# An FFN with per-batch mixing: two loads on another queue, one application moved into the next step, the last product regrouped by PSUM bank

## The chip, the core and the metric

The kernel runs on one core of a Trainium2 chip. A core has five engines that run their own instruction streams: TensorE (PE in the profile; its weight loads are PEld), VectorE (DVE), ScalarE (ACT), GpSimd (POOL) and SyncE (SP). SP only issues transfers here; ACT and POOL can issue them too. The metric is device time in microseconds of one launch. Before the change the median of three runs is 420.22 us (418.6 to 420.79).

## The reference

For every one of 64 batches a 64x64 matrix is picked by an index and applied across the channels; the result goes through a dense 1024x1024 layer and through a low-rank branch of the expert that a gate chooses for each token; the input is added at the end.

```python
W = weights[condition]                       # 64 of 16 matrices, each 64 x 64
h = einsum('bct,bcd->bdt', x, W)             # x: 64 x 64 x 1024
h = h.reshape(-1, 1024)                      # 4096 tokens
logits = h @ gate_w.T + expert_bias          # 4 experts
one_hot = onehot(argmax(logits))
base = h @ W_up.T
z = einsum('nh,erh->ner', h, lora_A)         # rank 8
delta = einsum('ner,ehr,ne->nh', z, lora_B, one_hot)
out = x + base + delta
```

All inputs and outputs are float32.

## The kernel before

The 4096 tokens are 32 pieces of 128 rows (two batches each). The picked matrices mix rows, and the dense weights mix columns, so the kernel does the weights first: u = x W for the joined weights W of 1024 x 1060 columns (4 gate columns, 32 of the experts' A, 1024 of W_up; `NW`, `G` = 36 is the first 36), and then, in PSUM tiles called `o`, the block-diagonal matrix `bd` of the two batches times u. This second product is the "application" (`apply`, `cond_u`). It is done in column pieces (`COLS`: 354, 354, 352); the first piece holds the gate columns, from which `gate` works out the chosen expert's 32 numbers `z` on DVE in six small instructions. `turn` transposes `z` on PE and splits it into `zt`, `delta` adds the low-rank part to an application's piece by one more matmul, and `evict` takes the piece out of PSUM. `finish(i, j)` is `apply`, `delta` and `evict` of piece j of token piece i.

Full float32 accuracy is made from reduced-precision operands: every operand is split into a high part (a copy on ACT: `ah`, `hB`, `hT`, `uh`) and a low part (a subtraction on DVE: `al`, `lB`, `lT`, `ul`), and each product is three matmuls: high x high, high x low, low x high.

Two token pieces a = 2g and b = 2g+1 are one group. W is cut into a 2 x 2 grid of blocks B11 to B22 (512 rows by 530 columns, `NB`), x of a group into A11, A12 (piece a) and A21, A22 (piece b). Groups 0 and 1 do the 8 block products as they are (`eight`); groups 2 to 15 do 7 products with sums of blocks (`seven`: S1 to S4 of A, T1 to T4 of B). A block product is four chunks k = 0 to 3 (`KH`) of six matmuls: three for columns 0 to 263 (`CUT`) and three for columns 264 to 529, in the two banks of a PSUM tile `c` (three tiles, `chain`). Two one-bank tiles `o` are left for applications and transposes (`place`).

The order of work on PE, DVE, ACT and POOL is the order in which the program is written (`InOrder`, line 41; nearly every instruction has that line). It is written as a list of block products per group, and hooks `at(s, k, fn, ...)`: after chunk k of product s (k = -1: ahead of it) fn's instructions are put in. Transfers that SP issues are ordered by the framework's scheduler.

Three places matter here.

- The start (lines 348 to 397). Group 0's A11 and A21 are loaded together, in two transfers of `load_halves` into a tile `xx`: chunk 0 (`ONE`, 128 KB) on ACT's queue, chunks 1 to 3 (`REST`, 384 KB) on SP's, which comes behind the two halves of chunk 0 of B11 (line 387) and ahead of the chunks 1 to 3 of B11 (`load_b`, line 139). Short dummy matmuls (`keep_warm`) stand ahead of chunk 0 and between chunks 0 and 1 and 1 and 2.
- The seam between group 1 and group 2. `apply(a, 0)` and `gate(a)` of group 1's piece a stand after the last chunk of the last product of group 1 (lines 551, 552); `u_of(pb, 0, ...)`, the split of piece b's u, ahead of group 2's first product (line 593), `turn` after its chunk 2, and `delta` and `evict` after chunk 0 of the second product.
- The end, group 15 (lines 659 to 707). Its order of products is such that only S4 x B22 is left for the columns 530 to 1059 of piece a. This product writes one two-bank tile `c["5"]`. In its hooks stand `turn(b)` and the pieces 0 and 1 of piece b; behind it come the sums for piece a's second half in two pieces (178 and 352 columns), and `finish(b, 2)`, `finish(a, 1)`, `finish(a, 2)`. For the last two token pieces (a = 30, b = 31) x is loaded ahead into the tile `y` (`load_y`), `evict` adds to it on DVE, and each of the six column pieces is stored by its own transfer on SP. For all other pieces `evict` copies on ACT, POOL issues a transfer that adds x into `y`, and SP stores the whole piece of 512 KB.

Of the kernel before, what the change touches and what calls it, by code (L numbers as in the profile page):

```python
# [17 lines left out]
KH = KC // 2  # L18
# [7 lines left out]
LEFT = 512 - CUT  # L26
COLS = ((0, 354), (354, 354), (708, 352))
WARM = 27
GATE = (("lg", E), ("mx", 1), ("sc", E), ("m2", 1), ("zm", ER))
# [15 lines left out]
def kernel(  # L45
# [140 lines left out]
    def chain():  # L186
        return psum.tile([P, 1024], F32, name="c", tag="c", bufs=3)

    def product(g, which, hooks):

        for k in range(KH):
            for c, a, b, first in which:
                h, lo = As[g, a]
                for o, n in (
                    (c[:, LEFT:512], slice(0, CUT)),
                    (c[:, 512 : LEFT + NB], slice(CUT, NB)),
                ):
                    for m, (l, r) in enumerate(((h, wh[b]), (h, wl[b]), (lo, wh[b]))):
                        tensor.matmul(
                            o,  # L200
                            l[:, k],
                            r[:, k, n],
                            start=first and k == 0 and m == 0,
                            stop=k == KH - 1 and m == 2,
                            skip_group_check=True,
                        )
            for kk, fn, *args in hooks:
                if kk == k:
                    fn(*args)

    def body(c):
# [19 lines left out]
    def u_of(i, hf, c):  # L231
        u_split(i, half(hf), body(c))

    def u_add(i, c, t):
        s = ts["u", i] = temp("usum")
        vector.tensor_add(s, body(c), t)
# [13 lines left out]

    def load_y(i):
        ys[i] = yp.tile([P, H], F32, name="y", tag="y")
        nc.sync.dma_start(ys[i], x[i])

# [15 lines left out]

    wide = []

    def place():
        if wide and wide.pop(0):
            return chain()[:, :512]
        return psum.tile([P, 512], F32, name="o", tag="o", bufs=2)
# [6 lines left out]

    def apply(i, j):
        c0, n = COLS[j]
        o = os_[i, j] = place()
        cond_u(o[:, :n], i, slice(c0, c0 + n))

    def ycols(j):
        c0, n = COLS[j]  # L290
        s = G if j == 0 else 0
        return slice(s, n), slice(c0 + s - G, c0 + n - G)
# [19 lines left out]

    def turn(i):
        zp = place()
        tensor.transpose(zp[: 3 * ER, :P], zs[i].rearrange("p a b -> p (a b)"), ident)
        zt = zs[i] = sp.tile([3 * ER, P], F32R, name="zt")
        scalar.copy(zt, zp[: 3 * ER, :P])
        p = slice(2 * ER, 3 * ER)
        vector.tensor_sub(zt[p], zp[p, :P], zt[p].bitcast(F32))

    def delta(i, j):
        s, d = ycols(j)
        tensor.matmul(
            os_[i, j][:, s], zs[i], b3[:, d], start=False, stop=True, skip_group_check=True
        )

    def evict(i, j):

        s, d = ycols(j)
        o = os_.pop((i, j))[:, s]  # L330
        if i >= NP - 2:
            vector.tensor_add(ys[i][:, d], o, ys[i][:, d])
            nc.sync.dma_start(out[i, :, d], ys[i][:, d])
            return
        if j == 0:
            ys[i] = yp.tile([P, H], F32, name="y", tag="y")
        scalar.copy(ys[i][:, d], o)
        if j == 2:
            pool.dma_start(ys[i], x[i], accum_op=ALU.add)
            nc.sync.dma_start(out[i], ys.pop(i))  # L340

    def finish(i, j):
        apply(i, j)
        delta(i, j)
        evict(i, j)
# [23 lines left out]
    ONE, REST = slice(0, 1), slice(1, KH)  # L369
    load_halves(scalar, 0, ONE)  # L370

    one = cpool.tile([P, 1], F32, name="one")
# [13 lines left out]
    for n in pieces:  # L386
        nc.sync.dma_start(t[:, n], part("B11", 0)[:, n])  # L387
    load_halves(nc.sync, 0, REST)
    for k in range(1, KH):
# [61 lines left out]
    def eight(g):  # L451
# [3 lines left out]
        def at(s, k, fn, *args):  # L455
            h[s].append((k, fn, *args))
# [6 lines left out]
        if g == 0:  # L463
            each(0, -1, load_b, "B12", range(KH))
            at(0, 0, keep_warm, 8)
            at(0, 0, split_a, g, "A11", REST)
# [58 lines left out]
        else:  # L525
# [24 lines left out]
            at(7, 0, sums, g + 1, "S4")  # L550
            at(7, 3, apply, a, 0)
            at(7, 3, gate, a)
            order = (
# [13 lines left out]
    def seven(g):  # L567
# [6 lines left out]
        def at(s, k, fn, *args):  # L574
            h[s].append((k, fn, *args))
# [9 lines left out]
        def gate_of_b():  # L585
            wide.append(True)
            o = place()
            cond_u(o[:, :G], b, slice(0, G))
            gate(b, o)
            u_split(b, slice(G, NB), ts["last"][:, G:])  # L590

        if g == 2:
            at(0, -1, lambda: u_of(pb, 0, cp["1"]))
            at(0, 2, turn, pa)
            at(1, 0, delta, pa, 0)
            at(1, 0, evict, pa, 0)
            at(1, 1, finish, pa, 1)
            at(1, 2, finish, pa, 2)
            for k in range(KH):
                at(1 + k, 3, split_b, "T4", k)  # L600
            at(1, 3, apply, pb, 0)
            at(1, 3, gate, pb)
            at(2, 3, turn, pb)
        else:
            at(0, -1, lambda: u_sum(pb, 0, cp["2"], ts["t1"]))
            at(0, 1, finish, pa, 1)
            at(0, 3, finish, pa, 2)
            at(1, 2, apply, pb, 0)
            at(1, 2, gate, pb)
            at(2, 2, turn, pb)  # L610
# [48 lines left out]
        else:  # L659
# [7 lines left out]
                ("3", "S1", "T1", True),  # L667
                ("5", "S4", "B22", True),
            )
# [12 lines left out]
            at(5, -1, first_of_b)  # L682
            at(5, 0, turn, a)
            at(5, 1, gate_of_b)
            at(5, 2, delta, a, 0)
            at(5, 2, evict, a, 0)
            at(6, -1, lambda: u_add(b, c["3"], ts["t7"]))
            at(6, -1, lambda: scalar.copy(us[b][0][:, half(1)], ts["u", b]))
            at(6, -1, lambda: keep_sum("t8", c["3"], "t6"))
            at(6, 0, turn, b)  # L690
            at(6, 0, lambda: u_low(b, half(1), ts["u", b]))
            for j in (0, 1):
                at(6, 2, finish, b, j)
        run(g, order, h, c)
        cs[g] = dict(c)
        if last:
            wide.extend((True, True, False))
            s = temp("usum")
            pieces = [slice(NB, 708), slice(708, NW)]
            for n in pieces:  # L700
                d = slice(n.start - NB, n.stop - NB)
                vector.tensor_add(s[:, d], body(c["5"])[:, d], ts["t8"][:, d])
                scalar.copy(us[a][0][:, n], s[:, d])
            for n in pieces:
                u_low(a, n, s[:, n.start - NB : n.stop - NB])
            for i, j in ((b, 2), (a, 1), (a, 2)):
                finish(i, j)

# [49 lines left out]
```

## Time and profile before

| | |
|---|---|
| median of three runs | 420.22 us |
| the profiled execution: its own time | 419.19 us |
| its span in the profile | 417.4 us |
| PE busy | 409.3 us (98%) |
| PEld busy | 406.6 us (97%) |
| DVE busy | 286.4 us (69%) |
| ACT busy | 186.4 us (45%) |
| POOL busy | 74.2 us (18%) |
| granted TensorE clock | 1.00 |
| read and written in HBM | 43.68 MB, 16.78 MB |

The span runs from the first to the last instruction that the profiler recorded; 1.8 us of the execution's time lie around it. All times of day below are microseconds from the span's start. In a row of the timeline the first number is the start, the second the duration (of the whole run of instructions if there are several, shown as x and a count), then the engine, the source line, the operation and its tiles (written <- read); in square brackets stands how long the engine sat idle before it and what ended that. A matmul's duration is from its issue until its result has drained; the next matmul is issued earlier (264 columns: 0.123 us later), so starts, not durations, are to be summed on PE.

### The profile page before, as it was taken

To read this page: it belongs to the slowest core of one execution; us is meant where nothing else is said; L and a number is where in the kernel's file an instruction comes from. 1 tells how busy PE (TensorE), PEld (TensorE's weight loads), DVE (VectorE), ACT (ScalarE), POOL (GpSimd) and SP (SyncE) were. 2 spreads that over 40 slices of the span, in tenths; PEclk is the share of its full clock that TensorE was granted. 3 is DMA by queue.
4 is the path that set the end of the run, shared out by engine and by line. 5 is a ranking of instruction groups with operands and counts; after the bars stand their busy time and mean duration, and the time that the engine had idled before them with its cause. 6 is when DMAs were issued, how large, how long until landed. Compare 5 with 4: busy or idle time off the path is not lost.

```text
span 417.4 us, 8151 instructions
## 1 busy us (share of the span) xinstructions
PE 409.3 (98%) x3195; PEld 406.6 (97%) x3195; DVE 286.4 (69%) x644; ACT 186.4 (45%) x418; POOL 74.2 (18%) x91
## 2 busy tenths in 40 slices
PE   6999999999999999999999999999999999999995
PEld 5999999999999999999999999999999999999994
DVE  4887685876757667676676767666676776767765
ACT  5747555453434445233453534335343444524521
POOL 5303512021020201102020020201102020020000
PEclk9999999999999999999999999999999999999999
DMA  7988983443655534564443555534365553474434
GB/s 247 321 281 208 236 204 74 113 142 118 177 132 133 122 80 155 133 176 121 103 123 102 172 133 153 124 82 145 116 178 133 128 121 83 157 197 113 91 63 151
DMA packets 25270, 60.99 MB, mean 146 GB/s; under 512 B 3248, under 2 KB 4784, under 8 KB 25232
## 3 DMA queue, kind: packets, MB, share of 16 engines
q1 hardware_dynamic: 18400, 41.39, 27.8%
q0 software_dynamic: 6560, 18.96, 26.7%
q8 instruction: 25, 0.41, 0.4%
q14 instruction: 13, 0.11, 0.1%
q10 hardware_dynamic: 272, 0.13, 0.1%
HBM read 43.68 MB, written 16.78 MB: 145 GB/s over the span
## 4 chain that ended last, share of the span: by engine, by line
PE 89%; DMA 3%; DVE 3%; issue 2%; ACT 1%; POOL 0%; SPq 0%; DVEq 0%; POOLq 0%; ACTq 0%
PE c L41 74%; PE o L41 15%; DMA wraw<-in_w_dram 3%; DVE lT L41 1%; POOL wraw L41 0%; ACT hT L41 0%; DVE S L41 0%; DVE al L41 0%; DVE ul L41 0%; ACT uh L41 0%; DVE usum L41 0%; DVE y L41 0%; SPq L387 0%; DVE lB L41 0%; DVE bd L41 0%
## 5 line engine op out<-in xcount | busy, mean ns | idle before, releaser
L41 PE MATMUL c<-hT,ah 128*128 128x264 f32 x480 | 139.8, 291 | 0.0
L41 PE MATMUL c<-hT,al 128*128 128x264 f32 x480 | 137.0, 286 | 0.0
L41 PE MATMUL c<-lT,ah 128*128 128x264 f32 x480 | 137.0, 285 | 0.0
L41 PE MATMUL c<-hB,ah 128*128 128x264 f32 (+1 forms) x432 | 124.3, 288 | 1.9 <-ACT hB L41 1.9
L41 PE MATMUL c<-lB,ah 128*128 128x264 f32 (+1 forms) x432 | 123.1, 285 | 0.4 <-DVE lB L41 0.4
L41 PE MATMUL c<-hB,al 128*128 128x264 f32 (+1 forms) x432 | 123.2, 285 | 0.0
L41 PEld LDWEIGHTS c<-lT,ah 128*128 128x128 f32 x480 | 90.9, 189 | 0.0
L41 PEld LDWEIGHTS c<-hT,ah 128*128 128x128 f32 x480 | 90.8, 189 | 0.0
L41 PEld LDWEIGHTS c<-hT,al 128*128 128x128 f32 x480 | 90.7, 189 | 0.0
L41 PEld LDWEIGHTS c<-hB,ah 128*128 128x128 f32 x432 | 81.6, 189 | 2.3 <-ACT hB L41 2.3
L41 PEld LDWEIGHTS c<-lB,ah 128*128 128x128 f32 x432 | 81.9, 189 | 0.8 <-DVE lB L41 0.8
L41 PEld LDWEIGHTS c<-hB,al 128*128 128x128 f32 x432 | 81.5, 189 | 0.0
L41 POOL DMA_DIRECT2D y<-in_x_dram x30 | 28.8, 959 | 283.9 <-ACT y L41 283.9
L41 ACT COPY y<-o 128x354 f32<-128x354 f32 (+2 forms) x90 | 39.7, 442 | 57.2 <-PE o L41 54.8
L41 ACT CAST uh<-usum 128x530 fp32r<-128x530 f32 (+4 forms) x44 | 27.1, 616 | 72.4 <-DVE usum L41 72.3
L41 DVE TENSOR_TENSOR al<-S,ah 128x512 fp32r<-128x512 f32 x56 | 38.5, 688 | 24.4 <-ACT ah L41 24.4
L41 DVE TENSOR_TENSOR al<-xh,ah 128x512 fp32r<-128x512 f32 x46 | 31.7, 689 | 29.9 <-ACT ah L41 29.9
L41 PE MATMUL o<-uh,bd 128*128 128x354 f32 (+1 forms) x188 | 45.7, 324 | 0.0
L41 DVE TENSOR_TENSOR ul<-usum,uh 128x530 fp32r<-128x530 f32 (+4 forms) x44 | 30.0, 683 | 18.8 <-ACT uh L41 18.8
L41 ACT CAST zt<-o 96x128 fp32r<-96x128 f32 x32 | 8.4, 261 | 75.4 <-PE o L41 75.2
L41 POOL DMA_INDIRECT wsel<-in_cw_dram,idx x32 | 34.6, 1081 | 11.6 <-issue 5.2
L41 ACT CAST ah<-S 128x512 fp32r<-128x512 f32 x56 | 34.9, 623 | 1.8 <-DVE S L41 1.4
(74 smaller groups left out, 461.0 us busy)
## 6 DMA issues: line engine op xcount, KB each, us to landing
xh<-in_xt_dram SPq DMA_DIRECT2D x60, 256.0 KB, 5.1
y<-in_x_dram POOLq DMA_DIRECT2D x30, 512.0 KB, 5.6
out_dram<-y SPq DMA_DIRECT2D x30, 512.0 KB, 2.9
wraw<-in_w_dram SPq DMA_DIRECT2D x23, 265.0 KB, 6.4
wraw<-in_w_dram POOLq DMA_DIRECT2D x8, 265.0 KB, 6.8
y<-in_x_dram SPq DMA_DIRECT2D x2, 512.0 KB, 4.5
xx<-in_xt_dram SPq DMA_DIRECT2D x1, 512.0 KB, 7.2
wsel<-in_cw_dram,idx POOLq DMA_INDIRECT x32, 5.0
```

Of the source, the lines that this page charges most:

```text
L41: return lambda *a, **k: self.tc.keep_in_program_order(fn(*a, **k))
```

## The change

- The start: `REST` of A11 and A21 goes on ACT's queue, right behind `ONE`. SP's queue then has chunks 1 to 3 of B11 right behind chunk 0. The eight dummy matmuls between chunks 0 and 1 become six.
- The seam: `apply(pa, 0)` and `gate(pa)` move behind chunk 0 of group 2's first product, `u_of(pb, 0)` with them (its place in the order of ACT and DVE stays), and `turn(pa)` from behind chunk 2 to behind chunk 3. On DVE the low part of `zt` now comes behind `al` of S1.
- The end: the last product is taken bank by bank: twelve matmuls of 264 columns into one `o` tile, then twelve of 266 into the other. Piece a is applied in four pieces (`LAST`: 354, 176, 264, 266 columns). Its first two are copied by ACT, POOL adds x to these 494 columns (`FIRST`) by a transfer, and SP stores them in one transfer, which stands ahead of the other five stores in SP's order. `turn(a)` goes from behind chunk 0 to behind chunk 1 of S1 x T1; `turn(b)` and the pieces of b use halves of the two-bank tiles.

```diff
+LAST = ((0, 354), (354, NB - 354), (NB, CUT), (NB + CUT, NB - CUT))
...
+    def product_by_bank(g, places, a, b, hooks):
+
+        for m, (o, n) in enumerate(zip(places, BANKS)):
+            for k in range(KH):
+                part_of_product(g, a, b, True, k, o[:, : n.stop - n.start], n)
+                for kk, fn, *args in hooks:
+                    if kk == KH * m + k:
+                        fn(*args)
...
     def load_y(i):
+
         ys[i] = yp.tile([P, H], F32, name="y", tag="y")
-        nc.sync.dma_start(ys[i], x[i])
+        d = slice(FIRST if i == NP - 2 else 0, H)
+        nc.sync.dma_start(ys[i][:, d], x[i][:, d])
...
-        if i >= NP - 2:
+        if i == NP - 1 or d.start >= FIRST and i == NP - 2:
             vector.tensor_add(ys[i][:, d], o, ys[i][:, d])
             nc.sync.dma_start(out[i, :, d], ys[i][:, d])
             return
-        if j == 0:
+        if i < NP - 2 and j == 0:
             ys[i] = yp.tile([P, H], F32, name="y", tag="y")
         scalar.copy(ys[i][:, d], o)
-        if j == 2:
+        if i == NP - 2 and j == 1:
+            n = slice(0, FIRST)
+            pool.dma_start(ys[i][:, n], x[i][:, n], accum_op=ALU.add)
+        elif j == 2:
...
     load_halves(scalar, 0, ONE)
+    load_halves(scalar, 0, REST)
...
-    load_halves(nc.sync, 0, REST)
...
-            at(0, 0, keep_warm, 8)
+            at(0, 0, keep_warm, 6)
...
-            at(7, 3, apply, a, 0)
-            at(7, 3, gate, a)
...
-            at(0, -1, lambda: u_of(pb, 0, cp["1"]))
-            at(0, 2, turn, pa)
+            at(0, 0, apply, pa, 0)
+            at(0, 0, gate, pa)
+            at(0, 0, lambda: u_of(pb, 0, cp["1"]))
+            at(0, 3, turn, pa)
...
-                ("5", "S4", "B22", True),
...
-            at(5, 0, turn, a)
+            at(5, 1, turn, a)
             at(5, 1, gate_of_b)
             at(5, 2, delta, a, 0)
             at(5, 2, evict, a, 0)
-            at(6, -1, lambda: u_add(b, c["3"], ts["t7"]))
-            at(6, -1, lambda: scalar.copy(us[b][0][:, half(1)], ts["u", b]))
-            at(6, -1, lambda: keep_sum("t8", c["3"], "t6"))
-            at(6, 0, turn, b)
-            at(6, 0, lambda: u_low(b, half(1), ts["u", b]))
-            for j in (0, 1):
-                at(6, 2, finish, b, j)
+            at(5, 3, lambda: finish(a, 1, ts["w"][:, 512:]))
...
+            z = chain()
+            turn(b, z[:, :512])
+            u_add(b, c["3"], ts["t7"])
+            scalar.copy(us[b][0][:, half(1)], ts["u", b])
+            keep_sum("t8", c["3"], "t6")
+            u_low(b, half(1), ts["u", b])
             s = temp("usum")
...
+            places = place(), place()
...
+            product_by_bank(
+                g,
+                places,
+                "S4",
+                "B22",
+                [
+                    (3, lambda: finish(b, 0, z[:, 512:])),
+                    (3, u_bank, 0),
+                    (5, lambda: finish(b, 1, chain()[:, :512])),
+                    (5, u_bank_low, 0),
+                ],
+            )
+            nc.sync.dma_start(out[a, :, :FIRST], ys[a][:, :FIRST])
+            u_bank(1)
+            finish(b, 2, chain()[:, :512])
+            u_bank_low(1)
+            finish(a, 2)
+            finish(a, 3)
```

`u_bank(m)` adds bank m to the kept sum `t8` on DVE and copies the high part on ACT; `u_bank_low(m)` makes the low part on DVE.

## The prediction

> **What bounds the kernel now.** I read the page's busy shares first, then the chain that ended last, PE's waits, and then the timeline around each wait.
>
> ```profile
> span 417.4 us, 8151 instructions
> PE 409.3 (98%) x3195; PEld 406.6 (97%) x3195; DVE 286.4 (69%) x644; ACT 186.4 (45%) x418; POOL 74.2 (18%) x91
> ...
> PE 89%; DMA 3%; DVE 3%; issue 2%; ACT 1%; POOL 0%; SPq 0%; DVEq 0%; POOLq 0%; ACTq 0%
> ```
>
> PE works nearly all the time at granted clock 1.00, and the change takes no real matmul away. So it can win only where PE stands still, and after PE's last matmul. PE's own waits, all of them:
>
> ```profile
> PE c L41 <- ACT hB L41: 1.9, 2, 1.6
> PE o L41 <- DVE one L41: 1.0, 1, 1.0
> PE o L41 <- DVE ul L41: 0.4, 1, 0.4
> PE c L41 <- DVE lB L41: 0.4, 1, 0.4
> PE c L41 <- ACT uh L41: 0.2, 1, 0.2
> ```
>
> The second is the launch. The first and fourth are the start, the third is the seam of groups 1 and 2 (at 60 us), the last the end. Each is touched by one part of the change. Everything from 61 to 400 us runs without a wait of PE.
>
> **Part 1, the start.** PE has done chunk 0 at 6.2 us and begins chunk 1 at 8.61, when ACT has made `hB`:
>
> ```profile
> 7.26 0.51 ACT L41 CAST ah<-xx 128x384 fp32r<-128x384 f32 x1 [2.48 <-DMA xx<-in_xt_dram]
> 7.93 0.63 ACT L41 CAST hB<-wraw 128x530 fp32r<-128x530 f32 x1 [0.16 <-DMA wraw<-in_w_dram]
> ```
>
> `REST` (issued at 1.65) lands at 7.25, chunk 1 of B11 (issued at 2.12) at 7.91. Both lie on SP's queue, and the stretches show the transfer engines far from full while they wait:
>
> ```profile
> 3.00:3.50 0.50, 0.50 (x7) 0.50 (x6) 0.00 (x0) 0.00 (x0) 0.50 (x3) 1.00 0.71 240
> 3.50:4.00 0.50, 0.50 (x6) 0.28 (x3) 0.01 (x1) 0.34 (x2) 0.50 (x3) 1.00 0.56 110
> 4.00:4.50 0.50, 0.23 (x2) 0.18 (x1) 0.48 (x2) 0.50 (x3) 0.50 (x6) 1.00 0.83 127
> 4.50:5.00 0.50, 0.42 (x2) 0.22 (x3) 0.50 (x3) 0.28 (x2) 0.30 (x1) 1.00 0.62 117
> 5.00:5.50 0.50, 0.50 (x5) 0.50 (x5) 0.28 (x2) 0.00 (x0) 0.00 (x0) 1.00 1.01 277
> ```
>
> (The last two columns are the engines' share and GB/s.) From 3.5 to 5.0 us they move 110 to 127 GB/s; from 6.5 on, 376 to 387. ACT's queue is empty in that time. Moved to it, `REST` is issued at 1.20 (behind `ONE`, 0.74 + 0.46) and chunk 1 at 1.65.
>
> Lower end of the gain: only the issue moves, 0.43 to 0.47 us, the duration of `REST`'s issue on SP. Upper end: two streams fill the gap. Chunk 0, `ONE`, `REST` and chunk 1 are 265 + 128 + 384 + 265 = 1042 KB; summed over the stretches they are through at about 6.45 us, 672 KB of them after 3.25; at 370 GB/s these take 1.8 us, to 5.1: 1.35 us earlier. Below zero: ACT takes `REST` ahead of `hB`, and if the four loads share the engines so that `REST` lands like the 512 KB load of the same tile (7.2 us after issue, 8.4), `hB` starts at 8.93 instead of 7.93: 1.0 us lost. I take 1.2: three loads are issued by then and the engines are half idle, so of all rows these point at the one queue itself, and the upper end is nearer. The second issue on ACT delays its table load (1.22 to 2.50) by 0.46, to 2.96; its first copy of data is at 3.66, so that costs nothing. The two dummy matmuls cost 0.11 us only if chunk 1 is ready before 6.9. Behind chunk 1 the nearest need is `lB` of B21's chunk 0 (done 12.9, used at 14.0), whose loads ride the same stream and come earlier with it.
>
> The Trainium skill ("DMA: Bandwidth & Descriptors", section "Issuing engines are not separate DMA queues") says that issuing on several engines saves only the sequencer's issue time, as all transfers run on the same 16 engines. By that rule this part is worth 0.45, and the sum at the end is 1.45 instead of 2.2.
>
> **Part 2, the seam.**
>
> ```profile
> 59.70 0.48 PE L41 MATMUL o<-uh,bd 128*128 128x354 f32 x2
> 60.56 0.43 PE L41 MATMUL o<-ul,bd 128*128 128x354 f32 x1 [0.38 <-DVE ul L41]
> 60.83 0.29 PE L41 MATMUL c<-hB,ah 128*128 128x264 f32 x1
> ```
>
> The application takes 59.70 to 60.83 = 1.13 us of PE, where one without a wait takes 0.49 (385.02 to 385.51). Behind chunk 0 (6 x 0.123 = 0.735) its `ul` matmul is due at 59.70 + 0.735 + 0.325 = 60.76; `ul` is there at 60.51. So 0.64 us go. Two things come back. `turn` now ends product 0 (63.13) and `delta` follows 0.85 later (0.115 for the transpose, 0.735 for a chunk); from transpose to `zt` took 0.90 (63.05 to 63.95) with DVE free, and now `al` of S1 is ahead of it until 63.7: about 0.1 of wait. Then `evict` copies that `o` tile later than PE wants it for `finish(pa, 1)`: ACT has the copy of `t` first (c's last result drains at 64.1, so it runs 64.17 to 64.77), the eviction ends at about 65.1, PE is due at 64.95: 0.2. Net 0.35; ends 0.64 (neither wait shows) and 0.1 (both double). The gate comes 0.1 later and its first user, `turn`, waits at 63.13 for a `z` done at 62.5: nothing.
>
> **Part 3, the end.** PE's last matmul is issued at 412.99, DVE's last `y` is
>
> ```profile
> 413.45 0.51 DVE L41 TENSOR_TENSOR y<-o,y 128x352 f32<-128x352 f32 x1
> ```
>
> and SP's last store is issued at 414.0. I follow the new order with before's durations, without the gains upstream. `turn(a)` waited for `z` at 403.14 (idle from 402.9); behind chunk 1 it does not: 0.25 won on PE. Product 5 ends at 405.70, `finish(a, 1)` at 406.12 (4 matmuls of 176 columns at some 0.1), where z of b is ready too (its gate, on DVE, is 0.07 later than before). Bank 0 is done at 407.72, `finish(b, 0)` 408.36, half of bank 1 409.10, `finish(b, 1)` 409.75, bank 1 410.49, `finish(b, 2)` 411.14. From here DVE sets the pace: low part of `zt` 406.9, the two sums of 530 (0.61 apart) from 407.2, `ul` 408.6, `y` 409.2, bank 0's sum 409.6, `y` 410.1, `ul` 410.55, bank 1's sum 410.9, `y` 411.5, `ul` 411.9 to 412.3, `y` 412.3, and the last `y` after the last `delta` at 412.8 to 413.2. That is 0.75 us before 413.96. The tail of stores is denser (five transfers within 2.3 us, 1.05 MB in all), which takes perhaps 0.1 back: 0.65 net. Ends: 0.85, and zero if the hand-offs of DVE, ACT and PE each cost a little more.
>
> The new store of 494 columns stands first in SP's order and waits for POOL's transfer; all five others queue behind it. ACT's second copy is done at 406.65, and POOL issues 0.3 later, at 406.95. The nearest row is the last such transfer of before:
>
> ```profile
> y<-in_x_dram POOLq DMA_DIRECT2D x1, 512.0 KB, 5.4
> ```
>
> It was issued at 401.14, and its data flowed from 403.4 to 406.1. With half the bytes: 2.2 to the first byte, 1.35 of data, 0.4 = 4.0 us, so 410.95. Six issues 0.37 apart put the last at 412.8 at the earliest, and its data are ready at 413.2: no cost. This cover ends when the transfer takes over 4.4 us. At 5.4 the last store is issued at 414.2, and the part wins nothing. The skill's same page (section "Anatomy of one DMA") gives 2.0 us plus the bytes at 436 GB/s for such a transfer, an estimate of 2.6 us here; for 512 KB it would give 3.2 where this trace shows 5.4, so the trace's row is used.
>
> **The sum.** 1.2 + 0.35 + 0.65 = 2.2 us. The profiled execution (419.19, 1.8 of it around the span) would take 417.0; it lies 1.0 below the median of the runs, and from that median, 420.22, I get 418.0.
>
> **The rivals.**
>
> 1. The second queue saves the issue time only. For it: `ONE`, on ACT's queue from 0.74 on, needed 2.9 us for 128 KB although little else was moving. Against: the half-empty engines. 0.45 + 0.35 + 0.65 = 1.45: 418.8.
> 2. `REST` suffers from sharing and lands at 8.4. For: it is the first that ACT needs, and chunks 1 to 3 now run beside it, not behind it. -1.0 + 0.35 + 0.65 = 0: 420.2.
> 3. The start's gain is lost at the seam. The chain that ended last runs through a POOL transfer of 8.1 us (41.79 to 49.91) and a DVE that is busy without a break from 55.8 to the `ul` at 60.51. If these do not come earlier with PE, all gain up to there is capped at 60.83 + 0.735 - 60.72 = 0.84, less 0.3: 0.55 + 0.65 = 1.2: 419.0. Against: POOL's issue at 41.2 follows ACT's work on PE's results, and the transfer engines were half idle at 28 to 32 us, so nothing older holds them.
> 4. The other side: POOL's addition lands late, and five stores stand behind it. In the crowded window from 30 to 62 us the same kind of transfer took
>
> ```profile
> y<-in_x_dram POOLq DMA_DIRECT2D x2, 512.0 KB, 9.7
> ```
>
> At 9.7 it lands at 416.65 and the last store is issued at 418.5 instead of 414.0: 4.5 - 1.2 - 0.35 = 2.95 slower, 423.2. From 5.2 us on the end loses; from 8.9 us on the whole is slower by over 0.5%. Against: at the end only stores run.
>
> **How the numbers follow.** 0.5% of the time is 2.1 us, about what a measurement of this kernel can tell from no change. Chances: forecast 0.53 (its own range 1.7 to 2.9 us, of which 0.07 lies within 0.5%), rival 1 0.18, rival 2 0.08, rival 3 0.06, rival 4 or something of its size 0.15. Faster by over 0.5%: 0.53 - 0.07 = 0.46. Within: 0.07 + 0.18 + 0.08 + 0.06 = 0.39. Slower: 0.15. The range goes from all upper ends (1.35 + 0.64 + 0.85 = 2.85, and 0.4 for the spread of the runs: 417.0) to rival 2 with 0.4 of spread (420.6); rival 4 is left out.
>
> **What would show it.** Part 1: `hB` of chunk 1 starts at about 6.7 instead of 7.93, and the stretches from 3.5 to 5.0 move over 250 GB/s. At about 7.5 it is rival 1, above 7.93 rival 2. Part 2: the wait on `ul` is gone, small ones on `zt` and on the `y` copy appear at 64 to 65 us (less the start's gain). Part 3: from the last product's first matmul to SP's last issue; SP's wait for POOL's transfer ends before DVE's second `y`. I am wrong if the start's gain does not reach 61 us, if POOL's last transfer takes over 4.4 us, or if PE shows a wait between 61 and 400 us.

## The result, and the profile after

| | before | after |
|---|---|---|
| median | 419.61 us (14 runs, 417.82 to 421.24) | 419.78 us (14 runs, 418.53 to 421.83) |
| ratio after / before | | 1.0009, 95% interval 0.9987 to 1.0031 |
| the profiled execution: its time, its span | 419.19, 417.4 us | 419.16, 417.4 us |

The change makes no difference that can be measured. The interval goes from 0.5 us faster to 1.3 us slower: the time lies inside the predicted range, and the gain of 2.2 us that was forecast is not there. The first lines of the page after, with the shares of the chain that ended last:

```profile
span 417.4 us, 8160 instructions
PE 409.8 (98%) x3197; PEld 407.1 (98%) x3197; DVE 285.6 (68%) x643; ACT 186.9 (45%) x420; POOL 75.5 (18%) x92
...
PE 90%; DMA 3%; DVE 2%; issue 2%; ACT 1%; POOL 0%; SPq 0%; POOLq 0%; DVEq 0%; ACTq 0%
```

and PE's waits (engine, tile and releaser: us in total, times, longest):

```profile
PE o L42 <- DVE one L42: 1.0, 1, 1.0
PE c L42 <- ACT hB L42: 0.8, 2, 0.4
PE c L42 <- DVE lB L42: 0.4, 1, 0.4
PE o L42 <- DVE ul L42: 0.3, 1, 0.3
```

The wait for `hB` went from 1.9 to 0.8, as part 1 meant. The wait for `ul`, which part 2 was to remove, is still there. (This list counts a wait from the modelled end of the matmul before; below, PE's waits are what lies between two starts beyond the usual distance.) To see where the 1.1 us of the start went, PE's timeline is cut at three matmuls that are the same in every version: number 100 and number 500 (counted from 0, without the dummies; about 20 and 71 us) and number 3080 (about 401 us, in the last group). From 500 to 3080 every execution but that of one variant takes 330.12 to 330.19 us, so all that differs is in three columns:

| | start: up to matmul 100 | seam: 100 to 500 | end: from 3080 to 0.05 us ahead of the span's end | span |
|---|---|---|---|---|
| before | 20.33 | 51.46 | 15.44 | 417.4 |
| after | 19.31 | 51.87 | 15.99 | 417.4 |
| difference | -1.02 | +0.41 | +0.55 | 0 |

**Start.** The stretches after (the last two columns are the transfer engines' share and GB/s) and ACT's timeline:

```profile
3.50:4.00 0.50, 0.50 (x6) 0.29 (x3) 0.00 (x0) 0.32 (x2) 0.50 (x3) 1.00 1.07 393
4.00:4.50 0.50, 0.19 (x2) 0.15 (x1) 0.47 (x2) 0.38 (x2) 0.50 (x6) 1.00 1.03 368
4.50:5.00 0.50, 0.42 (x2) 0.22 (x3) 0.40 (x2) 0.50 (x2) 0.30 (x1) 1.00 1.08 367
```

```profile
5.76 0.51 ACT L42 CAST ah<-xx 128x384 fp32r<-128x384 f32 x1 [0.73 <-DMA xx<-in_xt_dram]
6.91 0.63 ACT L42 CAST hB<-wraw 128x530 fp32r<-128x530 f32 x1 [0.64 <-DMA wraw<-in_w_dram]
```

The half-empty stretches are full, the split of `REST` starts 1.5 us earlier (5.76 for 7.26) and that of chunk 1 1.0 earlier (6.91 for 7.93).

**Seam.** PE's timeline at the application of group 1's piece a:

```profile
59.68 0.49 PE L42 MATMUL o<-uh,bd 128*128 128x354 f32 x2
60.50 0.43 PE L42 MATMUL o<-ul,bd 128*128 128x354 f32 x1 [0.33 <-DVE ul L42]
60.76 0.29 PE L42 MATMUL c<-hB,ah 128*128 128x264 f32 x1
```

PE arrives at 59.68, one chunk further on than before at 59.70, and waits for the same `ul` nearly as long as before: the second row starts 0.82 us after the first, 0.49 of that waiting (0.86 and 0.54 before).

**End.** SP's queue, and the last sum on DVE:

```profile
410.89 0.33 SPq L739 DMA_DIRECT2D out_dram<-y  x1
411.33 2.35 SPq L348 DMA_DIRECT2D out_dram<-y  x5
412.36 0.43 DVE L42 TENSOR_TENSOR y<-o,y 128x266 f32<-128x266 f32 x1 [0.26 <-PE o L42]
```

Counted from matmul 3080, the last `y` is ready at 11.45 (12.04 before), the last store is issued at 11.94 (12.11), and its data have landed at 14.69 (14.15). DVE's lead of 0.59 shrinks to 0.17 in SP's queue and turns into a loss of 0.54 behind the issue.

### The profile page after: what moved, and what is told of

It is laid out like the page before. It is cut to its first block, busy times and chain, and to the rows that moved or that the text cites. A ratio compares the mean times of both kernels' runs of the same rounds, so it can differ in the third digit from the quotient of the medians.

```text
span 417.4 us, 8160 instructions
## 1 busy us (share of the span) xinstructions
PE 409.8 (98%) x3197; PEld 407.1 (98%) x3197; DVE 285.6 (68%) x643; ACT 186.9 (45%) x420; POOL 75.5 (18%) x92
## 4 chain that ended last, share of the span: by engine, by line
PE 90%; DMA 3%; DVE 2%; issue 2%; ACT 1%; POOL 0%; SPq 0%; POOLq 0%; DVEq 0%; ACTq 0%
PE c L42 74%; PE o L42 16%; DMA wraw<-in_w_dram 3%; DVE lT L42 1%; POOL wraw L42 0%; ACT hT L42 0%; DVE S L42 0%; DVE al L42 0%; SPq L406 0%; DVE lB L42 0%; DVE ul L42 0%; ACT wraw L42 0%; DVE bd L42 0%; ACT hB L42 0%; DVE wraw L42 0%
## 5 line engine op out<-in xcount | busy, mean ns | idle before, releaser
L42 PE MATMUL c<-hB,ah 128*128 128x264 f32 (+1 forms) x424 | 122.0, 288 | 0.8 <-ACT hB L42 0.8
L42 PE MATMUL c<-lB,ah 128*128 128x264 f32 (+1 forms) x424 | 121.0, 285 | 0.4 <-DVE lB L42 0.4
L42 PE MATMUL c<-hB,al 128*128 128x264 f32 (+1 forms) x424 | 121.0, 285 | 0.0
L42 POOL DMA_DIRECT2D y<-in_x_dram x31 | 29.7, 958 | 288.4 <-ACT y L42 283.3
L42 PEld LDWEIGHTS c<-lB,ah 128*128 128x128 f32 x424 | 80.4, 190 | 1.0 <-DVE lB L42 0.8
L42 PEld LDWEIGHTS c<-hB,ah 128*128 128x128 f32 x424 | 80.1, 189 | 1.2 <-ACT hB L42 1.2
L42 PEld LDWEIGHTS c<-hB,al 128*128 128x128 f32 x424 | 80.1, 189 | 0.0
L42 ACT COPY y<-o 128x318 f32<-128x318 f32 (+2 forms) x91 | 40.1, 442 | 57.8 <-PE o L42 55.4
L42 PE MATMUL o<-uh,bd 128*128 128x354 f32 (+2 forms) x186 | 45.2, 324 | 0.0
```

Source lines behind the costliest of these rows:

```text
L42: return lambda *a, **k: self.tc.keep_in_program_order(fn(*a, **k))
```

## The experiments

Three questions: is each part's sign as in this pair of profiles; does the start's gain get lost at the seam in general (rival 3), or in this execution; and what of the end is lost to POOL's transfer, to the order of the stores, and to their size.

**The parts alone.** Part 1 alone:

```diff
     load_halves(scalar, 0, ONE)
+    load_halves(scalar, 0, REST)
...
-    load_halves(nc.sync, 0, REST)
...
-            at(0, 0, keep_warm, 8)
+            at(0, 0, keep_warm, 6)
```

> The kernel before with part 1 alone (REST on ACT's queue, six dummy matmuls). Mark used in all runs: the start of PE's first matmul of the last application of piece a's gate columns (before 400.94 us, after the change 400.36). Theory, the start's gain is lost at the seam: chunk 1 begins at about 7.6 us instead of 8.61, PE stands some 0.7 us earlier from 25 us on, but the ul matmul at the seam still starts at 60.5 and PE's wait for it grows from 0.38 to about 1.1 us; mark at 400.85 to 400.95. Rival, the start's gain passes the seam and something later takes it: ul matmul at about 59.8, mark at about 400.2.

Part 2 alone:

```diff
-            at(7, 3, apply, a, 0)
-            at(7, 3, gate, a)
...
-            at(0, -1, lambda: u_of(pb, 0, cp["1"]))
-            at(0, 2, turn, pa)
+            at(0, 0, apply, pa, 0)
+            at(0, 0, gate, pa)
+            at(0, 0, lambda: u_of(pb, 0, cp["1"]))
+            at(0, 3, turn, pa)
```

> The kernel before with part 2 alone. Theory, part 2 alone makes all of the change's gain up to 400 us, the start adds nothing to it: no wait for ul or one under 0.1 us, mark at 400.35 to 400.55 (after the change 400.36). Rival, start and seam both pay and a later stall takes a part of each: mark at 400.7 or later.

Part 3 alone is the changed kernel with these two diffs undone.

> The kernel before with part 3 alone; mark at 400.94 as before. Theory, the end's gain is lost behind the last instruction, in SP's row of stores and in their slow landing: DVE's last y starts at about 412.9 (before 413.45), SP's last store is issued at about 413.85 (before 414.03), it lands 2.7 us after its issue (before 2.04), and the span is 417.9, 0.5 longer than before. Rival, the stores land as before (2.0 us) and the end does gain: span 417.2.

| measured | start | seam | end | span |
|---|---|---|---|---|
| part 1 alone | 18.86 | 50.82 | 15.44 | 415.3 |
| part 2 alone | 20.57 | 51.06 | 15.44 | 417.3 |
| part 3 alone | 19.73 | 51.38 | 16.23 | 417.5 |

The times were 417.14, 419.04 and 419.32 us, one run each, beside 421.31 for one run of the kernel before on the same chip. The mark of the expectations fell at 398.87 with part 1 alone, far ahead of what theory and rival said; at 400.78 with part 2 alone, as the rival said; and at 400.25 with part 3 alone, where 400.94 was expected. The parts' own columns tell more than these single times. Part 1 alone carries its gain through the seam, although the seam has the old order there; PE's timeline has no wait:

```profile
58.23 0.48 PE L41 MATMUL o<-uh,bd 128*128 128x354 f32 x2
58.56 0.32 PE L41 MATMUL o<-ul,bd 128*128 128x354 f32 x1
58.72 0.28 PE L41 MATMUL c<-hB,ah 128*128 128x264 f32 x1
```

So the old order doesn't wait in every execution, and part 2 has less to remove than its one profile showed. Part 3 alone makes the end 0.79 longer: its sign is wrong without help from the others.

**A seam that is later still.** If the wait comes from arriving too early, one chunk more should remove it.

```diff
-            at(0, 0, apply, pa, 0)
-            at(0, 0, gate, pa)
-            at(0, 0, lambda: u_of(pb, 0, cp["1"]))
-            at(0, 3, turn, pa)
-            at(1, 0, delta, pa, 0)
-            at(1, 0, evict, pa, 0)
-            at(1, 1, finish, pa, 1)
-            at(1, 2, finish, pa, 2)
+            at(0, 1, apply, pa, 0)
+            at(0, 1, gate, pa)
+            at(0, 1, lambda: u_of(pb, 0, cp["1"]))
+            at(1, 0, turn, pa)
+            at(1, 1, delta, pa, 0)
+            at(1, 1, evict, pa, 0)
+            at(1, 2, finish, pa, 1)
+            at(1, 3, finish, pa, 2)
...
-            at(1, 3, apply, pb, 0)
-            at(1, 3, gate, pb)
+            at(2, 0, apply, pb, 0)
+            at(2, 0, gate, pb)
```

> The changed kernel with the moved application one chunk later still: apply, gate and the split of piece b's u behind chunk 1 of group 2's first product, the transpose behind chunk 0 of the second, delta and what follows one chunk later too. Theory, PE's wait for ul is what takes the start's gain, and nothing else near it does: no wait for ul, mark at 399.6 to 399.7 (after the change 400.36), span 416.7. Rival, DVE or the transfers hold PE at another place once this wait is gone: mark at 400.2 or later.

Measured: 419.55 us; start 18.85, seam 51.96, end 16.42. The `ul` wait at 60 us is gone, but `ul` was done at 60.22 here and PE came to the application at 60.61, so the order of part 2 would hardly have waited either. A wait of the same kind stands in another place, at group 0's application at 21 us (0.25, 0.10 and 0.44 us). It is not this variant's own: part 3 alone (0.44) and the timed variant with the store third (0.42, 0.10 and 0.46) have it too. The stretch behind matmul 500 is 330.50, 0.3 longer than in all others. The mark falls at 400.33, where the rival had it, and the variant wins nothing.

**What decides the wait at the seam.** All 14 profiled executions of this study, with old or new order, answer this together. The last of ACT's `hT` splits ahead of the seam that waits for a transfer starts 0.02 us after one load of T (issued by POOL) lands; from that start DVE is busy in a fixed sequence until `ul`. In before, after, and part 1 alone, from ACT's timeline:

```profile
49.93 0.64 ACT L41 CAST hT<-wraw 128x530 fp32r<-128x530 f32 x1 [1.32 <-DMA wraw<-in_w_dram]
```

```profile
49.86 0.64 ACT L42 CAST hT<-wraw 128x530 fp32r<-128x530 f32 x1 [1.24 <-DMA wraw<-in_w_dram]
```

```profile
47.38 0.64 ACT L41 CAST hT<-wraw 128x530 fp32r<-128x530 f32 x1 [0.21 <-DMA wraw<-in_w_dram]
```

and the `ul` that PE needs, from DVE's timeline of the same three:

```profile
59.81 0.70 DVE L41 TENSOR_TENSOR ul<-c,uh 128x530 fp32r<-128x530 f32 x1
```

```profile
59.74 0.70 DVE L42 TENSOR_TENSOR ul<-c,uh 128x530 fp32r<-128x530 f32 x1
```

```profile
57.26 0.71 DVE L41 TENSOR_TENSOR ul<-c,uh 128x530 fp32r<-128x530 f32 x1
```

From the start of `hT` to the end of `ul` are 10.58, 10.58 and 10.59 us; over all 14 executions it is 10.58 to 10.61. So `ul` is set by the landing of that load and by nothing that PE does from then on. And the landing varies against PE: it comes 28.1 to 31.0 us behind matmul 100, with either start. Whether PE waits, and for how long, is a race between the two that comes out anew in each execution.

The issue of the load does follow PE: POOL issues it 21.5 to 22.6 us behind matmul 100 in all 14. What varies most is the time from there to the landing, 6.6 to 8.8 us. From the chain that ended last (start, duration), before and after:

```profile
41.79 8.12 DMA wraw<-in_w_dram
```

```profile
41.02 8.82 DMA wraw<-in_w_dram
```

After the change the load was issued 0.77 us earlier and took 0.70 longer, so 0.07 were left. (The landing is counted in 16 steps in the trace: fifteen had come 7.27 and 6.89 us after the issue, and the last one alone at 8.12 and 8.82.) What makes this last step late was not found.

Where there is no wait over 0.2 us at 21 or at 60 us, the seam's stretch shows the cost of the order itself: 50.81 to 50.84 with the old order (three executions), 51.03 to 51.19 with the new (four). The 0.2 us are two small waits more, one ahead of `delta` (0.09 to 0.11, on `zt`) and one behind it (0.12 to 0.14), at 62 to 64 us in every execution with the new order. Against that, PE waits over 0.1 us for `ul` at 60 us in three of seven executions with the old order (0.44, 0.54 and 0.79) and in one of seven with the new (0.49). All waits included, the stretch takes 51.22 us on average with the old order and 51.49 with the new.

**The end.** Three variants of the changed kernel. Without POOL's addition for the 494 columns:

```diff
-            pool.dma_start(ys[i][:, n], x[i][:, n], accum_op=ALU.add)
+            pass
```

> The changed kernel without POOL's last addition: x is left out of 494 columns of token piece 30, and the first store no longer waits for a transfer. Theory A, the stores land late because all of them are issued and flow in one burst: now the first goes at about 406.5, the second at 409.3, the last at 412.85 when its data are ready; it lands 2.0 to 2.2 us after its issue (2.75 with the change), span 416.2 to 416.4 (417.4 with the change). Theory B, the small last stores land slowly by themselves, with rows of 1064 bytes: last issue 412.85, landing 2.7 later, span 416.9.

With all stores of the last pieces in the order in which they are written, so that the 494-column store is third:

```diff
-    tensor, vector, scalar, pool = (
-        InOrder(tc, e) for e in (nc.tensor, nc.vector, nc.scalar, nc.gpsimd)
+    tensor, vector, scalar, pool, sync = (
+        InOrder(tc, e) for e in (nc.tensor, nc.vector, nc.scalar, nc.gpsimd, nc.sync)
...
-            nc.sync.dma_start(out[i, :, d], ys[i][:, d])
+            sync.dma_start(out[i, :, d], ys[i][:, d])
...
-            nc.sync.dma_start(out[a, :, :FIRST], ys[a][:, :FIRST])
+            sync.dma_start(out[a, :, :FIRST], ys[a][:, :FIRST])
```

> The changed kernel with the 494-column store third in SP's order, behind the first two pieces of b. Theory A (burst): SP issues 409.3, 410.1, 410.9, 411.45, 412.15, 412.85; the last store is issued 0.43 earlier than with the change, and as the first two stores (340 KB) flow before the rest, it lands 2.2 to 2.4 after its issue; span 416.4 to 416.7. Theory B (small stores are slow by themselves): last issue 412.85, landing 2.7 later, span 416.9 to 417.0.

With that store on ACT's queue:

```diff
-            nc.sync.dma_start(out[a, :, :FIRST], ys[a][:, :FIRST])
             u_bank(1)
+            scalar.dma_start(out[a, :, :FIRST], ys[a][:, :FIRST])
```

> The changed kernel with the 494-column store on ACT's queue, behind ACT's last copy. The last store on SP at 412.85 as in the run with the store third; if two queues do not hinder each other, the landing is that of that run or up to 0.2 earlier, span 416.3 to 416.9. If the flow of bytes to memory is the limit, the queue makes no difference: within 0.1 us of that run.

The times were 417.11, 417.21 and 418.98 us, one run each, beside 418.17 for the kernel before. All from matmul 3080 on (the second execution of part 3 alone is from the timed runs below):

| | last `y` ready | last store issued | landed behind its issue | end |
|---|---|---|---|---|
| before, and four other executions with the old end | 12.04 | 12.11 | 2.03 | 15.44 |
| after | 11.45 | 11.94 | 2.75 | 15.99 |
| part 3 alone | 11.45 | 11.97 | 2.96 | 16.23 |
| part 3 alone, second execution | 11.48 | 11.80 | 2.94 | 16.04 |
| the later seam | 11.46 | 12.14 | 2.98 | 16.42 |
| without POOL's addition | 11.46 | 11.49 | 2.28 | 15.07 |
| 494-column store third | 11.45 | 11.48 | 2.40 | 15.18 |
| 494-column store on ACT's queue | 11.45 | 11.48 | 2.79 | 15.57 |

SP's waits in the last 13 us (line and releaser: us in total, times, longest), after:

```profile
SPq L739 <- DMA y<-in_x_dram: 4.3, 1, 4.3
SPq L789 <- DMA out_dram<-y: 2.3, 1, 2.3
```

before:

```profile
SPq L752 <- DMA out_dram<-y: 1.6, 1, 1.6
```

and in the variant with that store third:

```profile
SPq L789 <- DMA out_dram<-y: 2.0, 1, 2.0
...
SPq L42 <- DMA y<-in_x_dram: 0.6, 1, 0.6
```

L739 is the store of the 494 columns; it waits 4.3 us for POOL's transfer, and five stores behind it. L752 and L789 are the wait for the last store. In the four executions with this order POOL's transfer takes 4.21, 4.35, 4.38 and 4.55 us (part 3 alone, second execution; after; part 3 alone; the later seam), and the last store is issued 11.80, 11.94, 11.97 and 12.14 us behind matmul 3080: with a transfer 0.34 longer the last issue comes 0.34 later. These issues are 0.32 to 0.68 us behind the last store's data. When the first store no longer holds up the queue (third, on ACT's queue, no addition), it is 0.03: so the order of the stores costs 0.3 to 0.65 us.

What is left are 0.25 to 0.95 us more behind the last issue, and their cause is open. It is least where POOL's addition is left out; but the sizes differ from before there too (six stores as before, the last of 266 columns for 352, the big one of 494), and size, order and addition were not told apart. Theory A of the two expectations had 2.0 to 2.2 and 2.2 to 2.4 us, theory B 2.7; the 2.28 and 2.40 lie nearer to A, but two later executions with the store third took 2.61 and 2.85 (below), so they do not decide. On ACT's queue the big store is issued 1.45 us ahead of the last one, and the last lands 2.79 us behind its issue, neither of the two outcomes expected there, and as late as in the changed kernel: it isn't SP's queue alone that makes it late.

**The parts again, timed.** Part 1 alone, the variant with the store third, and part 3 alone, each in five rounds beside the kernel before on one chip (419.73 us, 35 runs):

> Part 1 alone, timed. In the looks so far the second matmul of chunk 1 (which waits for the low part lB) starts at 8.44 to 9.62 us with before's start (three executions) and at 7.87 to 9.41 with the changed start (six); the two late ones (9.62, 9.41) are the two in which the full clock was granted only at about 9 us. Theory 1, the start pays about 1.2 us when the clock comes early and 0.2 when it comes late, and nothing later takes it: ratio about 0.9975. Rival, what is won at the start is lost by 61 us in most executions: ratio 0.9995 to 1.0005.

> The changed kernel with the 494-column store third in SP's order, timed. Theory 1: start -1.0, seam +0.2 (the new places of transpose, delta and eviction wait a little in every execution), end -0.26 instead of +0.55 to +0.98: about 1.1 us faster than before, ratio 0.9975. Rival: the end's order is worth nothing outside the profile: ratio as the change's, 1.000 to 1.001.

> Part 3 alone, timed. Theory 2: the end costs 0.55 to 0.98 us in every execution (from the last product but one to the end of the span it took 15.44 us with before's end in three profiles, 15.99 to 16.42 with the changed end): ratio 1.0013 to 1.0023. Rival: 0.9985, the 0.5 us by which DVE is done earlier.

With them a version made from what the runs had shown: part 1, the old seam, the end with the store third, and on DVE the small `idx` behind the low part `lB` of chunk 1, which it had held up:

```diff
+            each(0, 0, split_b, "B11", (1,))
             at(0, 0, make_idx)
             for i in range(4):
                 at(0, 0, load_cond, i)
-            each(0, 0, split_b, "B11", (1,))
```

> Part 1, before's seam, part 3 with the 494-column store third, and the index computation (idx) behind lB of chunk 1 in DVE's order. Theory: lB no longer stands behind idx, which waits for the small matmul that PE does behind the dummy ones; the second matmul of chunk 1 follows the first by 0.25 to 0.45 instead of 0.75 to 1.03 us; the end is 0.26 shorter than before; 1.6 to 2.0 us faster than before, ratio 0.9955 to 0.996. Rival: the loads for the next chunks hold PE instead, waits at 11 to 14 us take the gain of idx: ratio as part 1 alone.

| | median, us | ratio to before | 95% interval | start | seam | end |
|---|---|---|---|---|---|---|
| part 1 alone | 418.75 | 0.9969 | 0.9948 to 0.9990 | 22.23 | 50.81 | 15.43 |
| store third | 418.50 | 0.9973 | 0.9950 to 0.9996 | 18.86 | 52.28 | 15.42 |
| part 3 alone | 420.25 | 1.0016 | 0.9994 to 1.0038 | 22.46 | 51.89 | 16.04 |
| the version from the parts | 418.19 | 0.9946 | 0.9927 to 0.9966 | 20.16 | 50.84 | 15.65 |

The ratio is not the quotient of the two medians; the two differ by up to 0.2%. By the ratio part 1 is worth 1.3 us (0.4 to 2.2), and part 3 costs 0.7 (from a gain of 0.3 to a loss of 1.6). The new end is 0.60 longer in part 3's second execution too (16.04 for 15.44). With the store third (this version among them) the end was 15.18, 15.42 and 15.65 in three executions, and the last store landed 2.40, 2.61 and 2.85 us behind its issue: on average what the old end takes. So even mended, part 3 shows no gain. The version from the parts is faster than the kernel before by 0.54% (0.34 to 0.73%), which is 2.3 us, where the medians lie 1.5 apart; that it beats part 1 alone is not shown, since the intervals overlap.

The kernel before, profiled a second time:

> The kernel before, unchanged, profiled once more. Theory, the wait for ul at the seam (0.38 us in the profile shown) and the landing of the first loads are not the kernel's but the execution's: no wait for ul at 60 us or another length, chunk 1 of group 0 begins somewhere from 7.6 to 8.7 us; the stretch from the last product but one to the end takes 15.44 us again. Rival, both are fixed: 0.38 and 8.61 again within 0.1.

Measured: 418.45 us; start 19.70, seam 51.36, end 15.44, span 416.7. PE waits for `ul` at 60 us again, 0.44 us for 0.54, so this wait, which the theory expected gone or of another length, came back much the same. The start did not: its `hB` of chunk 1 starts at 7.32; in the three others with the old start it is at 6.95 to 7.37. The profile that the prediction read, with 7.93, is the latest of the five.

**The start's gain and PE's pace.** The start column of the four timed kernels spreads from 18.86 to 22.46 for a reason of its own. Two executions with the same new start, PE's timeline, the end of chunk 0 and the beginning of chunk 1. Part 1 alone, first execution:

```profile
5.92 0.29 PE L41 MATMUL c<-hB,ah 128*128 128x266 f32 x1
6.05 0.28 PE L41 MATMUL c<-lB,ah 128*128 128x266 f32 x1
6.17 0.28 PE L41 MATMUL c<-hB,al 128*128 128x266 f32 x1
6.30 0.51 PE L41 MATMUL o<-warm 128*128 128x128 bf16 x6
6.74 0.19 PE L41 MATMUL o<-condf,batch 2*128 2x32 bf16 x1
6.86 0.39 PE L41 MATMUL c<-hB,ah 128*128 128x264 f32 x1
```

The timed one:

```profile
6.79 0.42 PE L41 MATMUL c<-hB,ah 128*128 128x266 f32 x1
7.01 0.42 PE L41 MATMUL c<-lB,ah 128*128 128x266 f32 x1
7.23 0.43 PE L41 MATMUL c<-hB,al 128*128 128x266 f32 x1
7.45 0.86 PE L41 MATMUL o<-warm 128*128 128x128 bf16 x6
8.25 0.20 PE L41 MATMUL o<-condf,batch 2*128 2x32 bf16 x1
8.38 0.59 PE L41 MATMUL c<-hB,ah 128*128 128x264 f32 x1
```

Starts are 0.12 us apart in the first and 0.22 in the second. `hB` was there by 6.6 in both (its split starts at 5.91 and 5.96); in the second PE itself comes too late for it. Eight dummies in place of six, at the same pace (part 2 alone, with the old start):

```profile
7.45 1.08 PE L41 MATMUL o<-warm 128*128 128x128 bf16 x8
8.46 0.20 PE L41 MATMUL o<-condf,batch 2*128 2x32 bf16 x1
8.59 0.59 PE L41 MATMUL c<-hB,ah 128*128 128x264 f32 x1
```

The clock column of the stretches reads 1.00 all the while; the trace's record of the granted clock begins with its first entry at full pace, and in the five late executions that entry falls between PE's last starts 0.22 apart and its first 0.12 apart. By it, full pace begins at 3.7 to 5.4 us in nine executions, at 8.7 to 10.0 in three (part 2 alone, the store on ACT's queue, the version from the parts), at 13.6 and 13.8 in two. Compared within these groups, the new start wins 0.96 (mean of six, 18.96, against mean of three, 19.92), 0.18 (on ACT's queue 20.39, part 2 alone 20.57) and 0.23 (22.23, 22.46). In the two late groups this gain is that of the two dummies less: chunk 1 begins at 8.38 with six in both and at 8.59 and 8.58 with eight, and the data were there before. At full pace the dummies are at most 0.11 of the 0.96 (from the first of them to the batch matmul behind them 0.55 with eight, before, and 0.44 with six). The dummies and the queue were not tried apart. The version from the parts, 20.16, is 0.23 ahead of the store on ACT's queue, although its full pace begins 1.3 later: its second matmul of chunk 1 starts at 8.72 for 9.41, since `lB` no longer waits for `idx`.

## Why the prediction was right or wrong

**Part 1, predicted 1.2.** Right in mechanism: the transfer engines fill up and the data come earlier. In size it lies within the timed interval (0.4 to 2.2). `hB` came at 6.91 where about 6.7 was predicted, in the eight other executions with the new start at 5.91 to 6.44; the stretches move 341 to 407 GB/s where over 250 was predicted. Rival 1, with the issue time only, is out: over all executions the split of chunk 1 starts at 6.18 with the new start (mean of nine) and at 7.31 with the old (mean of five), 1.13 us earlier. So is rival 2. (A third reading, that chunk 1 comes earlier since `REST` no longer stands ahead of it on SP's queue, was not tried by itself; by itself it gives no reason for `REST` to be split 1.5 us earlier, with an issue 0.45 earlier.) The rule of the Trainium skill ("DMA: Bandwidth & Descriptors", section "Issuing engines are not separate DMA queues") allowed the issue time alone; the measurement stands against it here, and decides. What the prediction did not see is that PE isn't always ready for the data: "The two dummy matmuls cost 0.11 us only if chunk 1 is ready before 6.9" is true at full pace alone. At half pace chunk 0, six dummies and the batch matmul end at 8.4, with eight dummies at 8.6: the earlier data win nothing there, and the 0.2 that are left come from the dummies. Weighted with how often each pace came (9 and 5 of 14) the start is worth about 0.7 us, an estimate; the 1.2 were right for the data and too much for PE.

**Part 2, predicted 0.35.** The step that failed is "So 0.64 us go": it took a wait of one execution as the kernel's own. `ul` is a load's landing plus 10.58 us, and that landing moves from execution to execution; four of the seven executions with the old order had no such wait at 60 us. The 0.3 that come back are there, 0.2 in size: the wait on `zt` as predicted, the one on the eviction not, and one behind `delta` in its place. Since the 0.64 are there in some executions alone and the 0.2 in all, the part is worth less than nothing wherever the load lands early. It also doesn't add to part 1, as the sum had it: in the profiled pair PE arrives 1.0 us earlier, the load lands only 0.07 earlier, and the wait is back. The two parts together bring 71.79 to 71.18 at matmul 500, 0.61 us, where rival 3 had said 0.55. Its condition held in this pair, that the chain to `ul` does not come earlier with PE, but not as something fixed: POOL's issue came 0.77 earlier, as the prediction held against this rival, and the transfer took 0.70 longer. So rival 3 describes this pair, but not the kernel: part 1 alone is 2.11 us ahead at the same matmul (69.68), more than its start's 1.47, because there the load landed 2.55 us earlier.

**Part 3, predicted 0.65.** The sign was wrong. DVE's pace was followed nearly rightly (0.59 for 0.75). The first step that failed is "Six issues 0.37 apart put the last at 412.8 at the earliest [...]: no cost". To compare with its times of day, 0.58 us have to be added to those of after, since matmul 3080 stands at 401.92 before and at 401.34 after. On that clock POOL's transfer was issued at 407.05 (406.95 worked out), took 4.35 us (4.0) and landed at 411.40 (410.95). The six issues were 0.48 apart (410.89 to 413.28 in five steps), not 0.37. So the last one came 0.49 behind its data, where the sum had 0.4 to spare, and 0.4 of DVE's lead went. The second step is "The tail of stores is denser [...], which takes perhaps 0.1 back": the last store landed 2.75 us behind its issue for 2.03 before, 0.7. Together -0.55 instead of +0.65. Rival 4 had the right place, five stores behind one transfer, and the wrong price. By it the end loses when the transfer takes over 5.2 us, and by the prediction the cover ends at 4.4; the end lost with transfers of 4.2 to 4.55, since the row of issues behind it is longer and the landing later. From the four executions the cover would end at about 3.9 us, an estimate: there the last issue would meet the 11.48 of the variants. The same page's section "Anatomy of one DMA" gives an estimate of 2.6 us for this transfer; the measured 4.35 does not agree.

**The sum.** By the runs it is about 1.0 for the start at full pace and 0.2 at half, -0.2 to -0.3 at the seam, and -0.55 to -0.98 at the end: nothing within 0.5 us, as measured. And of the 2.2 us between 420.22 and the forecast, 0.6 was the starting point: over 14 runs the kernel before takes 419.61. That the time lies within the stated range (417.0 to 420.6) owes something to luck: the range's upper end came from rival 2, whose mechanism did not occur, and the losses at the seam and the end that cancelled the start's gain were in no rival at this size.

## What to carry to other kernels

A wait in one profile is a race between two chains, and before it is costed its later chain should be followed back to what starts it: where that is a transfer's landing, the wait varies from execution to execution and counts as a gain only in the share of executions that have it, while what a reordering costs stays in all. At the end of a kernel count to the landing of the last store, not to its data: a store that waits at the head of a queue lets those behind it pile up, and here the issue spacing and the later landing of the last pieces cost more than DVE's earlier end was worth. Gains of parts that lie upstream of the same wait need not add.

## What the runs showed of the hardware

- With `REST` and B11 on one queue the transfer engines were not kept busy at the start, and by how much varied: from 3.5 to 5.0 us the old start moved 110 to 335 GB/s in five executions, the new one, with a second queue, 341 to 407 in nine of nine.
- PE's full pace was granted anywhere from 3.7 to 13.8 us after the start of nearly the same instructions, with dummies running from 1.0 us on. Matmul 100 falls at 18.85 to 20.33, 20.16 to 20.57 and 22.23 to 22.46 in the three groups. These 3.6 us are nearly as much as the spread of the runs (417.8 to 421.8 us), and more than any part of this change. What decides the moment was not tested.
- From issue to landing the last store takes 2.03 us with the old end in five executions; with the new end (as many stores, the last two smaller and one larger) 2.28 to 2.98 in nine.
- POOL's adding transfer took 4.2 to 4.8 us for 247 KB (eight executions) and 5.3 to 5.7 for 512 KB (14), both at the end with little else moving.
- The same load of 265 KB, issued by POOL at the same place of the program, took 6.6 to 8.8 us to land in 14 executions, with the transfer engines' mean share above 1.0 all that time.
